# Layer 0 edge loop of a graph kernel: one-hots turned by TensorE in place of a broadcast of places, and the steps of three groups staggered in a fixed order

## Chip, cores and metric

One core of one Trainium2 chip. The time is the device time of one execution in microseconds (us); a time quoted for a kernel is the median of its timed runs. "Same" means within 2%.

The kernel before was met in two states. In the first comparison, whose chip is not on record, it took 7032 to 7043 us (four timed runs); in the first profile and in every later call, on the chips numbered 3, 4, 6 and 9, it took 6512 to 6539. I call them the slow and the fast state (the names are mine: the record compares the runs of one call only, and marks all of them fast). Numbers are only compared within one state.

## The reference

Four graph layers follow one another; the change touches only the first, a graph attention layer over 4096 nodes with 65536 edges (plus one self loop per node), 8 heads of 64 features:

```python
def _L0_gnn_ref(x, edge_index, W, a):
    ...
    h = jnp.einsum('nc,hcf->hnf', x, W)
    s_src = jnp.einsum('hnf,hf->hn', h, a_src)
    s_dst = jnp.einsum('hnf,hf->hn', h, a_dst)
    e = s_src[:, :, None] + s_dst[:, None, :]
    e = jnp.where(e > 0, e, ALPHA * e)
    e = jnp.where(adj[None, :, :], e, NEG_INF)
    att = jax.nn.softmax(e, axis=-1)
    out = jnp.einsum('hij,hjf->hif', att, h)
    out = jnp.transpose(out, (1, 0, 2)).reshape(N, H * F)
    return jax.nn.softmax(out, axis=1)
```

The kernel doesn't build the dense `att`. It walks the edges, sorted by source node, in 544 tiles of 128 edges. For each tile it gathers the rows of the far nodes, weighs them with exp(score), and adds them up by source node with a matmul against a one-hot matrix.

## The kernel before

The tiles go in 68 groups of eight. Cut to what the argument needs:

```python
def fetch(g):                        # GpSimd: eight indirect gathers, 4 groups of buffers
    rows = ep.tile([P, GT, DA], F32, name="rows", bufs=4)
    for j in range(GT):
        gather(rows[:, j, :D + H], htab, s_dst[:, at(g) + j:at(g) + j + 1])
    return rows

def fetch_places(g):                 # SyncE: the places of 1024 edges, broadcast to all partitions
    places = ep.tile([P, GT * P], BF16, name="places", bufs=3)
    nc.sync.dma_start(places, loc_rows[at(g):at(g) + GT].rearrange("t c -> (t c)").partition_broadcast(P))
    return places

def source_parts(g, places):
    oh_t = ep.tile([P, GT * P], BF16, name="oh_t")
    nc.vector.tensor_scalar(oh_t, places, col_i, None, op0=OP.is_equal)      # transposed one-hots
    e_ps = eps.tile([P, GT, 2, H], F32, name="e_ps")
    ...                              # ScalarE: four small copies `of`; PE: 24 score matmuls oh_t x of
    return e_ps

def weights(g, rows, u):             # DVE: the weights go into the row itself, then the one-hots
    nc.vector.tensor_mul(rows[:, :, D:D + H], u, s_new[...])
    return one_hots(ep, s_loc, at(g), GT)

def weigh(j, rows):                  # two heads on ScalarE, six on DVE
    two = rows[:, j:j + 2]
    ...
    g = two[:, :, :VH * F].rearrange("p t (h f) -> p t h f", h=VH)
    nc.vector.tensor_mul(g, g, two[:, :, D:D + VH].unsqueeze(3).to_broadcast([P, 2, VH, F]))

for g in range(-3, groups):
    ...                              # fetch(g+3), fetch_places(g+2), source_parts(g+1)
    for j in range(0, GT, 2):
        weigh(j, rows[g])
        if ps is not None:
            keep(g, j - 2, ps)       # DVE: acc += sum_ps
        ps = add_up(g, j, rows[g], done[g])      # PE: eight sum matmuls into sum_ps (two buffers)
        if j == 2:
            u = scores(rows[g + 1], e_ps)
    done[g + 1] = weights(g + 1, rows[g + 1], u)
    keep(g, GT - 2, ps)
```

`weigh` reads the rows and the weights. `one_hots` compares `row_i` with `s_loc`.

## Time and profile before

| | kernel before |
|---|---|
| timed, slow state | 7043.11 us (3 runs), with the run added later 7040.15 (4 runs) |
| profiled span, fast state | 6523.0 us, granted clock 0.966 |
| layer 0 loop, start of the first to start of the last gather | 277.5 to 1027.8: 750 us |

The lines of the profile that matter are in the prediction. A line of the groups view reads: line, engine, operation, names, shapes, count; then busy us and the mean ns of one; then idle time ahead of it and what ended that idle time.

### The profile page before, as it was taken

How to read it: one execution, taken by the hardware profiler on the slowest of the kernel's cores; microseconds unless marked ns; L12 is line 12 of the kernel's file. 1: busy time of each engine (PE TensorE's matmuls, PEld its weight loads, DVE VectorE, ACT ScalarE, POOL GpSimd, SP SyncE). 2: the span in 40 equal slices, each digit the busy share in tenths (PEclk: the TensorE clock that was granted, in tenths of full speed). 3: DMA queues.
4: the chain of work that ended last, by engine and by line, in shares of the span. 5: the costliest groups of instructions: out<-in, count | busy, mean ns of one | idle time of the engine just before them, and what ended most of it. 6: DMA issues, size and time to landing. Idle time of an engine off the chain costs nothing. (4 is left out here: it accounts for less than half of the span.)

```text
span 6523.0 us, 65629 instructions
## 1 busy us (share of the span) xinstructions
PE 5718.0 (88%) x18462; PEld 2778.4 (43%) x18462; DVE 4141.7 (63%) x7141; ACT 2937.3 (45%) x3977; POOL 3254.1 (50%) x3324
## 2 busy tenths in 40 slices
PE   6678887888779799999999999999999889978885
PEld 4366664322224344444444444444444365532221
DVE  7577778455443376676676776776766545556665
ACT  3244444300011277777777777777777533300001
POOL 1277772477760365555555555555555100037774
PEclk9899999999899899999999999999999899989998
DMA  8777775566774333333333333333333211137777
GB/s 225 182 220 214 218 215 176 162 201 203 195 214 175 125 109 103 102 98 104 101 98 105 101 98 102 103 98 106 100 98 104 82 45 62 59 106 209 210 209 243
DMA packets 399757, 926.39 MB, mean 142 GB/s; under 512 B 135926, under 2 KB 135926, under 8 KB 399382
## 3 DMA queue, kind: packets, MB, share of 16 engines
q0 software_dynamic: 230976, 721.66, 37.6%
q1 hardware_dynamic: 168406, 200.39, 9.6%
q8 instruction: 155, 2.54, 0.2%
q14 instruction: 220, 1.80, 0.1%
HBM read 818.71 MB, written 103.11 MB: 141 GB/s over the span
## 5 line engine op out<-in xcount | busy, mean ns | idle before, releaser
L438 PE MATMUL m_ps<-w_sb,h_t 128*128 128x512 f32 x4224 | 1905.9, 599 | 31.2 <-ACT h_t L957 31.2
L803 PE MATMUL sum_ps<-g,oh 128*128 128x512 f32 x2144 | 1146.9, 636 | 218.1 <-DMA g<-ztab,d_src 80.2
L438 PEld LDWEIGHTS m_ps<-w_sb,h_t 128*128 128x128 f32 x4224 | 771.1, 190 | 983.6 <-issue 791.2
L449 POOL DMA_INDIRECT qg<-qtab,eg x528 | 504.0, 954 | 990.6 <-ACT h_t L957 845.7
L449 POOL DMA_INDIRECT g<-ztab,d_src x528 | 501.4, 950 | 866.4 <-issue 811.6
L459 DVE TENSOR_TENSOR acc<-acc,sum_ps 128x512 f32 x800 | 550.2, 688 | 546.4 <-PE sum_ps L803 541.4
L803 PEld LDWEIGHTS sum_ps<-g,oh 128*128 128x128 f32 x2144 | 336.9, 191 | 1015.4 <-DVE acc L459 388.5
L449 POOL DMA_INDIRECT g<-ytab,s_dst x544 | 536.9, 987 | 353.2 <-DMA ytab<-acc 185.6
L914 POOL DMA_INDIRECT eg<-aug,d_eid x528 | 569.0, 1078 | 242.4 <-issue 131.0
L449 POOL DMA_INDIRECT rows<-htab,s_dst x544 | 585.9, 1077 | 204.9 <-issue 138.9
L957 ACT COPY h_t<-tr_ps 128x512 f32<-128x512 f32 x528 | 283.6, 589 | 777.6 <-PE tr_ps L955 777.6
L735 PE MATMUL sum_ps<-rows,oh 128*128 128x261 f32 x2176 | 551.5, 410 | 60.3 <-PE sum_ps L735 41.2
L449 POOL DMA_INDIRECT pg<-ptab,eg x528 | 508.7, 963 | 160.9 <-issue 160.6
L735 PEld LDWEIGHTS sum_ps<-rows,oh 128*128 128x128 f32 x2176 | 427.3, 202 | 163.3 <-PE sum_ps L735 66.3
L967 PE MATMUL small_ps<-z,oh 128*128 128x512 f32 x1056 | 477.8, 595 | 8.4 <-DVE z L1027 8.4
L1006 DVE TENSOR_TENSOR z<-m_ps,b_bc 128x512 f32<-128x512 f32 x132 | 91.3, 692 | 467.3 <-PE m_ps L438 467.3
L459 DVE TENSOR_TENSOR acc<-acc,small_ps 128x512 f32 x528 | 361.1, 684 | 31.8 <-PE small_ps L967 4.3
L1165 ACT ACTIVATE acc<-acc,dis 128x512 f32<-128x512 f32 x32 | 19.7, 706 | 671.2 <-DVEq L464 671.2
L1027 DVE TENSOR_TENSOR z<-z,t 128x1024 f32<-128x1024 f32 x264 | 310.4, 1217 | 8.2 <-ACTq L464 4.8
L992 DVE TENSOR_TENSOR z<-m_ps,b_bc 128x512 f32<-128x512 f32 x132 | 91.3, 692 | 352.6 <-PE m_ps L438 352.6
L967 PEld LDWEIGHTS small_ps<-z,oh 128*128 128x128 f32 x1056 | 201.5, 191 | 263.7 <-issue 221.9
L955 PEld LDWEIGHTS tr_ps<-ident,pg 128*128 128x128 f32 x2112 | 248.0, 142 | 151.1 <-issue 120.0
(248 smaller groups left out, 8389.5 us busy)
## 6 DMA issues: line engine op xcount, KB each, us to landing
aug<-row SPq DMA_DIRECT2D x32, 560.0 KB, 3.9
places<-loc_rows SPq DMA_DIRECT2D x68, 256.0 KB, 3.8
xt<-in_x_dram SPq DMA_DIRECT2D x16, 1024.0 KB, 5.7
row<-in_edge_attr_dram SPq DMA_DIRECT2D x32, 512.0 KB, 6.6
x<-xt SPq DMA_DIRECT2D x16, 1024.0 KB, 4.3
xt<-x SPq DMA_DIRECT2D x16, 1024.0 KB, 7.5
rows<-htab,s_dst POOLq DMA_INDIRECT x544, 3.8
g<-ytab,s_dst POOLq DMA_INDIRECT x544, 3.7
```

Source lines behind the costliest of these rows:

```text
L438: nc.tensor.matmul(ps, h_t[:, k, :], w_sb[:, k0 + k, :], start=start and k == 0, stop=stop and k == KC - 1)
L449: nc.gpsimd.indirect_dma_start(out=dst_ap, out_offset=None, in_=table, in_offset=bass.IndirectOffsetOnAxis(ap=idx, axis=0))
L459: nc.vector.tensor_add(into, into, ps)
L735: nc.tensor.matmul(ps[:, c, :HW], oh[:, j + k, :], rows[:, j + k, c * HW:(c + 1) * HW], start=k == 0, stop=k == 1)
L803: nc.tensor.matmul(ps, oh[:, j + k, :], g[:, j + k, :], start=k == 0, stop=k == pair - 1)
L914: nc.gpsimd.indirect_dma_start(out=eg[:, j // 2, (j % 2) * HALF:(j % 2 + 1) * HALF], out_offset=None, in_=aug.rearrange("e c -> (e c)").un ...
L955: nc.tensor.transpose(h_ps[:, k, :], h[:, j, k * P:(k + 1) * P], ident)
L957: nc.scalar.copy(h_t, h_ps)
L967: nc.tensor.matmul(ps, oh, m, start=True, stop=True)
L992: nc.vector.tensor_add(zz[:, 0, :], ps, b2_bc)
L1006: nc.vector.tensor_add(zz[:, 1, :], ps, b2_bc)
L1027: nc.vector.tensor_mul(mz[:, j:j + 2], mz[:, j:j + 2], t[:, j:j + 2])
```

## The change

The intent: no broadcast of places from memory and no second compare on DVE. PE turns the one-hots that exist anyway (they have to be made two groups ahead for that), ScalarE copies the result out of PSUM. So that the longer way doesn't stand in line, the steps of three groups are interleaved in one fixed order. The core of the diff (the removal of `loc_rows` and `col_i`, and a class that this loop doesn't call, are left out):

```diff
-            def fetch_places(g): ...
-            def source_parts(g, places):
-                oh_t = ep.tile([P, GT * P], BF16, name="oh_t")
-                nc.vector.tensor_scalar(oh_t, places, col_i, None, op0=OP.is_equal)
+            def turn(oh):
+                made = []
+                for j in range(0, GT, 4):
+                    t_ps = eps.tile([P, 4, P], F32, name="t_ps")
+                    for k in range(4):
+                        nc.tensor.transpose(t_ps[:, k, :], oh[:, j + k, :], ident)
+                    made.append(t_ps)
+                return made
+            def turned(g, made):
+                oh_t = ep.tile([P, GT, P], BF16, name="oh_t")
+                for j, t_ps in enumerate(made):
+                    nc.scalar.copy(oh_t[:, 4 * j:4 * j + 4, :], t_ps)
...
-            def weigh(j, rows):
+            def weigh_last(j, rows):          # the two heads on ScalarE, now a step of their own
...
-            for g in range(-3, groups): ...   # the order shown above
+            for g in range(-3, groups + 1):   # (the tests for the first and last groups are left out)
+                rows[g + 3] = fetch(g + 3)
+                made = turn(ohs[g + 1])
+                weigh(0, rows[g]);      sums[0] = add_up(g, 0, rows[g], ohs[g])
+                weigh_last(2, rows[g]); weigh(2, rows[g])
+                keep(g - 1, 6, sums.pop(6))
+                parts = turned(g + 1, made)
+                sums[2] = add_up(g, 2, rows[g], ohs[g])
+                weigh_last(4, rows[g]); weigh(4, rows[g]); keep(g, 0, sums.pop(0))
+                ohs[g + 2] = one_hots(ep, s_loc, at(g + 2), GT, 3)
+                e_ps = source_parts(*parts)
+                sums[4] = add_up(g, 4, rows[g], ohs[g])
+                u = scores(rows[g + 1], e_ps)
+                weigh_last(6, rows[g]); weigh(6, rows[g]); keep(g, 2, sums.pop(2))
+                sums[6] = add_up(g, 6, rows[g], ohs[g])
+                weights(g + 1, rows[g + 1], u); weigh_last(0, rows[g + 1])
+                keep(g, 4, sums.pop(4))
```

## The prediction

> **What bounds the kernel now.** The change touches only the edge loop of layer 0, so I first asked the view by tile where that loop stands. Its gathers of `rows` start between 277.5 and 1027.8 us of a profiled span of 6523.0 us; its last matmul starts at 1048.4. So at most some 770 us can move, and 2% of the timed 7043 us is 141 us, over a sixth of that. The loop handles 544 tiles as 68 groups of eight, and a group now takes (1027.8 - 277.5) / 543 x 8 = 11.05 us.
>
> Next the groups by line between 281 and 1040 us (count, then busy us, mean ns, and idle time before with what ended it):
>
> ```profile
> L449 POOL DMA_INDIRECT rows<-htab,s_dst x542 | 584.0, 1077 | 165.1 <-issue 138.6 <-PE sum_ps L735 9.4 <-DMA rows<-htab,s_dst 5.2
> L735 PE MATMUL sum_ps<-rows,oh 128*128 128x261 f32 x2144 | 544.0, 410 | 58.5 <-PE sum_ps L735 41.2 <-issue 7.6 <-PE e_ps L701 0.2
> L729 DVE TENSOR_TENSOR rows<-rows 128x768 f32<-128x768 f32 x268 | 249.8, 952 | 0.0
> L742 DVE TENSOR_TENSOR acc<-acc,sum_ps 128x522 f32 x268 | 186.1, 694 | 154.4 <-PE sum_ps L735 153.9
> L701 PE MATMUL e_ps<-of,oh_t 128*128 128x16 bf16 x1632 | 52.1, 170 | 114.4 <-DVE oh_t L693 103.7 <-DMA places<-loc_rows 10.5 <-ACT of L698 0.2
> L693 DVE TENSOR_SCALAR oh_t<-places,col_i 128x1024 bf16<-128x1024 bf16 x67 | 36.4, 543 | 0.0
> ```
>
> GpSimd's busy and idle time add up to 584.0 + 165.1 = 749.1 us: it is never free, because its idle time is the same 0.30 us after every gather (165.1 / 542). PE and DVE stand idle in turns: DVE 154 us for the sums, PE 104 us for `oh_t`. That is a chain through both engines, not one full engine.
>
> The timeline of one undisturbed group shows how the two fit (start, us, engine, what, idle time before):
>
> ```profile
> 327.89 0.94 POOL L449 DMA_INDIRECT rows<-htab,s_dst  x1 [0.30 <-issue]
> ...
> 328.18 1.22 DVE L444 TENSOR_TENSOR oh<-row_i,s_loc 128x1024 f32<-128x1024 f32 x1
> ...
> 329.32 0.69 DVE L742 TENSOR_TENSOR acc<-acc,sum_ps 128x522 f32 x1
> 329.93 0.54 DVE L693 TENSOR_SCALAR oh_t<-places,col_i 128x1024 bf16<-128x1024 bf16 x1
> 330.39 1.81 DVE L729 TENSOR_TENSOR rows<-rows 128x768 f32<-128x768 f32 x2
> 330.50 0.32 SPq L687 DMA_DIRECT2D places<-loc_rows  x1
> ...
> 330.52 1.62 POOL L449 DMA_INDIRECT rows<-htab,s_dst  x1 [0.30 <-issue]
> 330.52 0.76 PE L701 MATMUL e_ps<-of,oh_t 128*128 128x16 bf16 x24 [1.37 <-DVE oh_t L693]
> ...
> 331.43 3.76 PE L735 MATMUL sum_ps<-rows,oh 128*128 128x261 f32 x16
> 332.45 0.95 POOL L449 DMA_INDIRECT rows<-htab,s_dst  x1 [0.30 <-issue]
> 333.46 0.70 DVE L742 TENSOR_TENSOR acc<-acc,sum_ps 128x522 f32 x1 [1.27 <-PE sum_ps L735]
> ```
>
> Two things are to be seen. A gather takes 0.95 us, so 1.25 us from start to start and 10.0 us for eight; but the one that starts when SyncE has just issued the broadcast of `places` takes 1.62. This comes once in nearly every group I looked at (607.21, 641.52, 653.10, 663.78): GpSimd's plain group is 10.0 + 0.67 = 10.67 us. And the chain of PE and DVE has almost the same length: from `oh_t` at 652.39 and 663.19 the next turn is 10.8 us later, and inside it DVE waits 1.27 us for the first sum and 0.66 us for the third. The loop has two bounds of equal length. A change to one alone would give nothing; this change takes something from both.
>
> **What the Trainium skill says.** "DMA: Bandwidth & Descriptors", section "SWDGE vs HWDGE vs iDMA": descriptors of a DMA issued from GpSimd are computed in software by GpSimd itself, those of a DMA issued from SyncE by hardware; its part "Issuing engines are not separate DMA queues" says that both run on the same 16 DMA engines and interleave. The trace agrees as far as it goes: the broadcast costs GpSimd no instruction, yet the gather beside it takes 1.62 in place of 0.95 us. "TensorE: Matmul & The Clock Gate", "Part 4: PE-mode transpose": a 128x128 transpose takes about 275 ns in a kernel, its result goes to PSUM and needs a copy out. The transposes of layer 2 in this trace (L955) have a median of 273 ns, and pipelined 224.4 us / 1731 = 0.130 us each. The same page, "Part 1: The HAM clock gate": the PE clock falls to half after an idle window of some 3.4 us. Here the granted clock was 0.96 at 330 to 500 us and 0.94 at 500 to 900.
>
> **The change part by part.**
>
> *Removed.* 68 broadcasts of 256 KB: a group moves eight gathers of 128 x 520 x 4 bytes, 2.13 MB, and 0.26 MB of places, so 11% of the traffic goes. On GpSimd 68 x 0.67 = 46 us of stretched gathers go, and its floor falls to 10.0 us a group. On DVE 68 x 0.54 = 37 us of `oh_t` go. The one store of places in the sort (160 KB, one DVE cast) is under 1 us, off any wait that counts.
>
> *Added.* PE: 544 transposes x 0.130 = 71 us, 1.04 us a group. ScalarE: 136 copies of 128x512 out of PSUM; L957 in layer 2 is the same copy, 0.587 us, so 80 us, 1.17 a group. ScalarE has 347 us of work in 760, so the engine has room; whether the copies stand in a chain is a matter of order.
>
> *Moved.* The one-hots are made two groups ahead, transposes one group ahead; `keep` of a pair runs one or two pairs after its sum, the last in the next turn. I walk the new order with the spacings of the old timeline: a DVE `weigh` 0.89 us (0.87 to 0.91 start to start), `keep` 0.61 (0.70 until its end), one-hots 1.14, four score steps 0.87, weights 0.15; on PE eight sum matmuls 1.88 (3.76 / 2), turn 1.04, 24 score matmuls 0.76; 0.15 from PE to DVE and 0.1 back. DVE alone: 4 x 0.89 + 4 x 0.61 + 1.14 + 0.87 + 0.15 = 8.2 us. PE alone: 4 x 1.88 + 1.04 + 0.76 = 9.3 us. GpSimd: 10.0. The longest ring through the order: turn 1.04, sum 0 1.88, sum 2 1.88, score matmuls 0.76, to DVE 0.15, scores 0.87, weigh 6 0.89, keep 2 0.70, to PE 0.10, sum 6 1.88, and the next turn begins: 10.15 us. `keep 2` is in it because `sum_ps` has two buffers and sum 6 takes that of sum 2. Beside it, ScalarE's exp, filler copy and last weighting after the scores (0.26 + 0.19 + 1.01) end at nearly the same time as keep 2, so they are close to being in the ring too. The `oh_t` copies end some 2.4 us after the transposes, while PE does 3.76 us of sums: hidden.
>
> The same walk of the old order (oh_t to score matmuls 0.59, those and the gap 0.91, sum 1.88, to DVE 0.15, keep 0.62, scores 0.87, weigh 0.95, sum 4 1.98, to DVE 0.2, keep 0.6, weights 0.2, one-hots 1.14, keep 0.61) gives 10.7, which is what the trace has. So the plain group goes from 10.7 to about 10.2 us, the larger of 10.15 and 10.0.
>
> *Sum.* The mean group is 11.05, 0.36 over plain, from half-clock stretches of PE and gathers that stretch around them (612.89 to 618.52: 1.22, 1.58, 1.92 us). I keep that 0.36: 10.55. Saved: 0.50 x 68 = 34 us, if timed runs behave like the profiled one. They don't quite: they took 7043 where the profiled run took 6525, and no view tells why. If PE was slower in them, the new ring, with 7.4 us of PE in 10.2 (the old one with some 4.4 us in 10.7), loses more; I take a little off and say 31 us: 7012.
>
> **The rivals.**
> 1. *GpSimd and the gathers are the whole bound, and PE and DVE follow.* For: no free time on GpSimd, data that come just in time at the start (DVE waited 9.9 us for the first). Then a group is 10.0 + 0.36, or better since 11% of the traffic is gone: 0.7 x 68 = 47 us, about 6995. Against: DVE waited for `rows` only 6 times, 14.2 us in all.
> 2. *PE becomes the bound.* Its share goes from 8.3 to 9.3 us of a group, and at half clock every piece of the new ring doubles. With PE 20% slower the ring is 10.15 + 1.5 = 11.6, the old one 11.6 as well: no gain, 7043, or a few us of loss. Against: granted clock 0.94 and more here; and a denser PE should have fewer idle windows.
> 3. *The stagger meets an order fault*: ScalarE's last weighting after the scores, or the wait of keep 0 on the first sum, adds 0.5 us a group. Then 7040 to 7060.
>
> **Range and chances.** All of these lie within 20 to 60 us of one another, because 68 groups can each give at most some 1 us: faster by 2% would need 2.1 us a group, below GpSimd's floor of 10.0, and slower by 2% would need a group of 13.1. The range goes from rival 1 with some clock gain (6975) to no gain (7045). Faster 0.03, within 2% 0.95, slower 0.02.
>
> **What would show it.** Right: no gather of 1.62 us at a regular distance; GpSimd now idle for something other than issue, as buffers come free late; group pitch 10.3 to 10.7 us; the transposes near 0.13 us each; DVE idle about 2 us a group, before the scores and keep 0; last matmul of the loop near 1015 in place of 1048. Rival 1: pitch 10.4 with GpSimd still never free. Rival 2: PE above 90% busy in the loop and a lower granted clock. Rival 3: ScalarE named as the releaser of the sum matmuls. What would make me wrong: stretched gathers that stay without the broadcast, or a loop that moves by over 60 us either way.

## The result

Ratios here are the mean time of one kernel's fast runs over that of the other's of the same rounds, so they are not quite the ratio of the medians.

The changed kernel took 7233.11 us (7221.04 to 7255.48, four runs) against 7040.15 us (7032.43 to 7043.34, four runs): ratio 1.0279, 95% interval 1.0253 to 1.0306. It is slower, where I had given that a chance of 2%.

This comparison was made in the slow state. Later calls put both kernels on other chips. There the change took 6544.84 against 6528.68 us (1.0027, 1.0011 to 1.0044) and 6545.62 against 6520.28 (1.0041, 1.0012 to 1.0070): within 2%, but slower by some 20 us, and not faster by the 31 that I had predicted. So two questions have to be kept apart: why the expected gain is missing in the fast state, and what takes 193 us in the slow one. The experiments settle the first; the second stays open.

The change in the slow state, groups by line over its layer 0 loop (281 to 1370 us):

```profile
L772 PE MATMUL sum_ps<-rows,oh 128*128 128x261 f32 x2176 | 627.8, 443 | 346.4 <-issue 283.4 <-remote 59.4 <-PE sum_ps L772 2.1
L473 POOL DMA_INDIRECT rows<-htab,s_dst x544 | 556.4, 1023 | 550.7 <-PE sum_ps L772 358.8 <-issue 141.7 <-DVE node L684 43.4
...
L741 DVE TENSOR_TENSOR u<-e_ps,rows 128x64 f32<-128x64 f32 x68 | 15.3, 225 | 337.9 <-remote 260.8 <-PE sum_ps L772 56.0 <-DMA rows<-htab,s_dst 12.9
```

The same view of the same kernel in the fast state (281 to 1060 us):

```profile
L473 POOL DMA_INDIRECT rows<-htab,s_dst x539 | 606.2, 1125 | 164.3 <-issue 134.4 <-PE sum_ps L772 18.0 <-DMA rows<-htab,s_dst 4.0
L772 PE MATMUL sum_ps<-rows,oh 128*128 128x261 f32 x2143 | 547.4, 405 | 143.1 <-issue 125.7 <-PE sum_ps L772 9.2 <-DVE rows L766 8.2
...
L766 DVE TENSOR_TENSOR rows<-rows 128x768 f32<-128x768 f32 x270 | 251.3, 952 | 0.0
L779 DVE TENSOR_TENSOR acc<-acc,sum_ps 128x522 f32 x267 | 185.7, 696 | 88.2 <-PE sum_ps L772 86.3 <-DVE rows L751 1.0
L715 PE MATMUL t_ps<-ident,oh 128*128 128x128 f32 x535 | 82.0, 304 | 0.0
...
L723 ACT CAST oh_t<-t_ps 128x512 bf16<-128x512 f32 x134 | 73.0, 588 | 64.4 <-PE t_ps L715 64.0
```

Compare the fast-state POOL row with that of before in the prediction (584.0 us busy, mean 1077 ns, 165.1 idle). GpSimd is as full as it was: the idle time is again 164.3 / 539 = 0.30 us after every gather and nothing else. But the mean gather has grown from 1077 to 1125 ns, though the broadcast that I blamed for the long gathers is gone. In the slow state GpSimd waits 359 us for buffers, and DVE 261 us for a semaphore that the profile can't name ("remote").

The span of the loop says the same. Tile view, gathers of `rows`: count, shortest, median and longest in ns, start of the first and of the last. First the kernel before in the fast state:

```profile
L449 POOL DMA_INDIRECT rows<-htab,s_dst x544: 942/946/1941, 277.5 to 1027.8; - x182
```

The change in the fast state:

```profile
L473 POOL DMA_INDIRECT rows<-htab,s_dst x544: 942/949/1767, 274.6 to 1050.4; - x182
```

And the change in the slow state:

```profile
L473 POOL DMA_INDIRECT rows<-htab,s_dst x544: 940/946/1987, 280.0 to 1342.7; - x182
```

That is 750, 776 and 1063 us. In the fast state the loop loses 26 us and the rest of the kernel gains about 10, which leaves the 16 us of the first pair of medians.

### The profile page after: what moved, and what is told of

Same layout as the page of the kernel before. It is cut to its first block, busy times and chain, and to the rows that moved or that the text cites. A ratio compares the mean times of both kernels' runs of the same rounds, so it can differ in the third digit from the quotient of the medians.

```text
span 7253.6 us, 66642 instructions
## 1 busy us (share of the span) xinstructions
PE 5883.1 (81%) x19006; PEld 3015.2 (42%) x19006; DVE 4118.4 (57%) x7072; ACT 3030.9 (42%) x4113; POOL 3286.2 (45%) x3323
## 5 line engine op out<-in xcount | busy, mean ns | idle before, releaser
L858 PEld LDWEIGHTS sum_ps<-g,oh 128*128 128x128 f32 x2144 | 447.8, 220 | 1140.5 <-issue 611.6
L772 PE MATMUL sum_ps<-rows,oh 128*128 128x261 f32 x2176 | 627.8, 443 | 346.4 <-issue 283.4
L473 POOL DMA_INDIRECT rows<-htab,s_dst x544 | 556.4, 1023 | 550.7 <-PE sum_ps L772 358.8
L969 POOL DMA_INDIRECT eg<-aug,d_eid x528 | 589.7, 1117 | 244.3 <-issue 128.6
L772 PEld LDWEIGHTS sum_ps<-rows,oh 128*128 128x128 f32 x2176 | 459.6, 220 | 455.0 <-issue 280.0
L473 POOL DMA_INDIRECT pg<-ptab,eg x528 | 550.2, 1042 | 167.6 <-issue 160.6
L1061 DVE TENSOR_TENSOR z<-m_ps,b_bc 128x512 f32<-128x512 f32 x132 | 91.3, 692 | 476.4 <-issue 405.5
L779 DVE TENSOR_TENSOR acc<-acc,sum_ps 128x522 f32 x272 | 189.6, 697 | 182.2 <-PE sum_ps L772 169.1
```

Source lines behind the costliest of these rows:

```text
L473: nc.gpsimd.indirect_dma_start(out=dst_ap, out_offset=None, in_=table, in_offset=bass.IndirectOffsetOnAxis(ap=idx, axis=0))
L772: nc.tensor.matmul(ps[:, c, :HW], oh[:, j + k, :], rows[:, j + k, c * HW:(c + 1) * HW], start=k == 0, stop=k == 1)
L779: nc.vector.tensor_add(into, into, ps[:, :, :HW])
L858: nc.tensor.matmul(ps, oh[:, j + k, :], g[:, j + k, :], start=k == 0, stop=k == pair - 1)
L969: nc.gpsimd.indirect_dma_start(out=eg[:, j // 2, (j % 2) * HALF:(j % 2 + 1) * HALF], out_offset=None, in_=aug.rearrange("e c -> (e c)").un ...
L1061: nc.vector.tensor_add(zz[:, 1, :], ps, b2_bc)
```

## The experiments

Thirteen runs. All gave correct results.

### The two kernels again, on other chips

Edit: none. First the kernel before.

> The kernel before, unchanged, profiled again. Theory A (two states of the chip or of the recording: the first profile, 6523 us, was taken in a state in which the timed runs, 7040 us, never were): about 7040 us, clock near 0.91, sums and scores that wait several us longer than their matmuls last, semaphore records lost as in the profile after, and the unchanged loops of layers 1 and 3 as long as in the profile after (784 and 845 us from first to last gather, against 711 and 661 in the first profile). Its layer 0 loop is then some 190 us shorter than the 1063 us of the changed kernel. Theory B (the change itself slows everything): 6523 us again.

Measured: 6525.91 us, span 6524.1, clock 0.968; seven runs of the kernel before on that chip (number 9) lie between 6521.33 and 6529.88. The time of 7040 belongs to the first comparison (its chip, or something else about that call), not to the kernel alone.

Then the change.

> The changed kernel again, in the hope of a chip in the state of the first profile of before (before at 6523 us, clock 0.97). Theory A (the 190 us come from the order of steps, to which the state only adds): about 6600 to 6700, a group of 12 to 13.5 us, no semaphore records lost and no wait without a releaser. Theory B (the loss belongs to the state alone: PE's results reach the other engines several us late there, which the new order meets more often in its ring): before 6523, this about 6490, a group near 10.5 us, as predicted. If before is at 7040 again: 7233 again, and nothing is told apart.

Measured (chip 6): 6544.84 us (6537.62 to 6552.35) against 6528.68, ratio 1.0027. The 2.8% did not come back; they need the slow state.

### One part of the change alone

Turning by TensorE, but the steps in the old order:

```diff
-            for g in range(-3, groups + 1): ...   # staggered
+            for g in range(-3, groups):
+                parts = turned(g + 1, turn(ohs[g + 1]))
+                for j in range(0, GT, 2):
+                    weigh(j, rows[g])
+                    ...                            # keep(j - 2), add_up(j), as before
+                    if j == 0: e_ps = source_parts(*parts)
+                    if j == 2: u = scores(rows[g + 1], e_ps)
```

> The steps in the old order, one-hots made a group earlier and turned by TensorE in place of the broadcast. If the turning (PE work, ScalarE copies, one more hop between engines) costs the 190 us: about 7200 or more. If the stagger does: about 7000 to 7040.

Measured: 6694.21 us against 6523.34, ratio 1.0258 (1.0241 to 1.0275); the loop takes 900 us. The timeline of one group (start, us, engine, what, idle time before it) shows why:

```profile
599.91 0.23 ACT L695 COPY of<-node 128x48 bf16 x1 [0.44 <-issue]
...
600.86 0.23 ACT L695 COPY of<-node 128x48 bf16 x1 [0.72 <-issue]
601.00 2.02 ACT L727 ACTIVATE rows<-rows 128x64 f32<-128x64 f32 x8
...
601.63 1.19 PE L736 MATMUL sum_ps<-rows,oh 128*128 128x261 f32 x4 [2.16 <-ACT rows L727]
...
602.85 0.70 DVE L743 TENSOR_TENSOR acc<-acc,sum_ps 128x522 f32 x1 [3.69 <-PE sum_ps L736]
```

In this trace ScalarE does its work in the order of the program: the two copies out of PSUM and the four `of` copies stand ahead of the weighting of two heads (L727), and the first sum matmul waits for that. This group loses 2.2 us on PE and 3.7 on DVE there; over the loop PE waits 127.5 us for these rows. Turning is only cheap if the order hides it, and that is what the stagger is for.

The stagger alone, with the broadcast and the compare on DVE kept:

```diff
-                for j, t_ps in enumerate(made):
-                    nc.scalar.copy(oh_t[:, 4 * j:4 * j + 4, :], t_ps)
+                nc.vector.tensor_scalar(oh_t..., places, col_i, None, op0=OP.is_equal)
...
-                    made = turn(ohs[g + 1])
+                    places[g + 2] = fetch_places(g + 2)
```

> The staggered order of the changed kernel, but with the broadcast of places and the DVE comparison, no turning. If the stagger costs the 190 us: about 7200. If the turning does: about 7000 to 7050.

Measured: 6573.70 us, ratio 1.0072 (1.0055 to 1.0089); the loop takes 808 us. The groups view of its loop:

```profile
L481 POOL DMA_INDIRECT rows<-htab,s_dst x544 | 643.7, 1183 | 209.2 <-issue 133.5 <-ACT of L729 43.7 <-PE sum_ps L774 14.9
```

The 43.7 lie before the first gather. So GpSimd is again never free, yet its mean gather is 1183 ns, the longest of all. The new order makes gathers longer, with the broadcast or without it. That sent me back to the gathers.

### What makes a gather long

In the prediction I took the long gather to be slowed by the broadcast that SyncE issues beside it. In the change there is no broadcast. Its gathers in the fast state, beside the DVE work around them:

```profile
606.92 0.95 DVE L766 TENSOR_TENSOR rows<-rows 128x768 f32<-128x768 f32 x1
...
607.12 1.58 POOL L473 DMA_INDIRECT rows<-htab,s_dst  x1 [0.30 <-issue]
...
609.00 0.95 POOL L473 DMA_INDIRECT rows<-htab,s_dst  x1 [0.30 <-issue]
609.21 1.82 DVE L766 TENSOR_TENSOR rows<-rows 128x768 f32<-128x768 f32 x2
610.25 1.60 POOL L473 DMA_INDIRECT rows<-htab,s_dst  x1 [0.30 <-issue]
...
611.74 0.95 DVE L766 TENSOR_TENSOR rows<-rows 128x768 f32<-128x768 f32 x1
...
612.15 1.35 POOL L473 DMA_INDIRECT rows<-htab,s_dst  x1 [0.30 <-issue]
```

The first weigh ends at 606.92 + 0.95 = 607.87, and the gather that started inside it ends at 608.70, 0.83 us later. The second gather that started inside a weigh ends at 611.85, 0.82 after the end of the pair (611.03); the third at 613.50, 0.81 after 612.69. The gather at 609.00, which was under way when a weigh began, takes its plain 0.95.

Over the whole loop of this run I sorted the 544 gathers by the DVE operation under way at their start. Of the 172 that started inside a weigh, 90% end 0.81 to 0.82 us after the end of the weigh (5th to 95th percentile), with a mean duration of 1.395 us. The 67 that started in the one-hots have a mean of 1.147, the 145 in `keep` 0.963, the 131 with DVE idle 0.947. Of before: 123 in a weigh, mean 1.438; 66 in the one-hots, 1.097; 144 in `keep`, 0.946; 153 idle, 0.946. What the two bad operations have in common is that both inputs lie in SBUF.

That is not the only way to hold a gather. In the run with the stagger alone, five gathers started while nothing but the `oh_t` compare ran on DVE, which reads one tensor from SBUF. They too end 0.82 us after it, and the longest took 1.12 us (at 435.03). In the kernel before no gather started so.

The Trainium skill has this, on pages that the prediction did not use. "SBUF — State Buffer", section "SBUF: two separate sides", says that VectorE and GpSimd share a port pair as an exclusive lock for the whole instruction, taken among others by a VectorE operation with two SBUF inputs against a GpSimd operation that reads SBUF (the gather takes its row numbers from `s_dst`, in SBUF); "GPSIMD Engine Reference", section "1. Specifications", names the contention in a line of its table. The trace agrees, with the 0.82 us beside it. In the old timeline the end of `oh_t`, the broadcast's issue (330.50) and the start of a weigh (330.39) fall together in each group, so that the wrong one could be blamed.

The theory can be tried from both sides. First the broadcast: double it, in the kernel before, the second copy unread.

```diff
                 nc.sync.dma_start(places, loc_rows[...].partition_broadcast(P))
+                again = ep.tile([P, GT * P], BF16, name="again", bufs=2)
+                nc.sync.dma_start(again, loc_rows[...].partition_broadcast(P))
```

> The kernel before with the broadcast of places sent twice, the second copy read by nobody. The step of the prediction (the broadcast stretches the gather beside it by 0.67 us): two stretched gathers a group, 117 us of stretch in place of 71, a group of 11.7 us, 6570 where before is at 6525. Theory C: stretch 71 us and 6525, within 10 us.

Measured: 6568.22 us, ratio 1.0068 (1.0051 to 1.0085). It costs 43 us, but not in the gathers. Groups view, and from the view of waits the one that is new (us in total, times, longest):

```profile
L449 POOL DMA_INDIRECT rows<-htab,s_dst x544 | 574.6, 1056 | 253.9 <-issue 140.8 <-PE sum_ps L737 52.8 <-ACT of L700 44.1
```

```profile
DVE oh_t L695 <- DMA places<-loc_rows: 39.3, 6, 11.9
```

The mean gather is 1056 ns, shorter than the 1077 of before. Most of the 43 us are six waits of `oh_t` for `places` that came late, 39.3 us in all, five of them at 382 to 455 us. A broadcast costs something when it comes late; it doesn't stretch gathers.

Now the other side: take the second SBUF input away. The weights are written to spare room of the `e_ps` bank too, and weigh reads them from there. In the change:

```diff
-                e_ps = eps.tile([P, GT, 2, H], F32, name="e_ps")
+                e_ps = eps.tile([P, 3, GT, 2 * H], F32, name="e_ps")
...
+                w = e_ps[:, 1, :, :H]
+                nc.vector.tensor_mul(w, u, s_new[...])          # beside the same product into rows
...
-                nc.vector.tensor_mul(g, g, two[:, :, D:D + VH].unsqueeze(3).to_broadcast([P, 2, VH, F]))
+                nc.vector.tensor_mul(g, g, w[:, j:j + 2, :VH].unsqueeze(3).to_broadcast([P, 2, VH, F]))
```

> The changed kernel, with the weights of the heads read from PSUM by the DVE multiplication of the rows, in place of from SBUF; same work, same order. Theory C (a gather that starts while DVE runs an operation with two inputs in SBUF is held up; in the profiles a gather that starts in the multiplication of the rows is stretched by 0.46 us on the mean, one that starts in a sum out of PSUM by 0.00): the stretched gathers go from 97 us in all to 15 to 30 us (the one-hots keep theirs), a group from 11.4 to 10.3 to 10.6 us, and 6470 to 6500 us where before is at 6525. Theory D (the stretch comes from something else, DMA traffic or the granted clock): 6545 as before. Should the chip be one where before takes 7040, the shares of stretched gathers still tell.

Measured: 6489.42 us (6485.32 to 6492.99) against 6524.89, ratio 0.9949 (0.9932 to 0.9965). That is "same" by the 2% rule, but clear of noise it is faster than both kernels, though it has one more DVE operation a group. Tile view of its gathers:

```profile
L473 POOL DMA_INDIRECT rows<-htab,s_dst x544: 942/946/1994, 280.1 to 1000.0; - x182
```

The loop takes 720 us in place of 776. All of the 137 gathers that start in a weigh take 0.94 to 0.95 us; the 64 that start in the one-hots take 1.539 on average.

The same edit in the kernel before (its one-hots and order unchanged):

> The same edit in the kernel before. Theory C with the second bound of my prediction (PE and DVE need 10.7 us a group in the old order anyway): stretched gathers from 71 to under 25 us, but only 0.3 to 0.4 us a group saved: 6498 to 6510 where before is at 6525. If GpSimd is the only bound: 10.3 us a group, 6475. Theory D: 6525.

Measured: 6543.96 us (6529.33 to 6560.84), ratio 1.0041 (1.0020 to 1.0062). Groups view of its loop:

```profile
L449 POOL DMA_INDIRECT rows<-htab,s_dst x541 | 527.6, 975 | 204.7 <-issue 141.1 <-PE sum_ps L737 51.0 <-DMA rows<-htab,s_dst 6.1
```

The gathers did get shorter, 975 ns for 1077, and by their starts the loop goes from 750 to 735 us. But that is not a gain. GpSimd only runs further ahead, and now waits for buffers that PE's sums free (51.0 us). By its sums the loop is as long as before. Tile view of the kernel before, then of this run:

```profile
L735 PE MATMUL sum_ps<-rows,oh x2176: 381/383/782, 294.9 to 1048.4; 128*128 128x261 f32 x198
```

```profile
L737 PE MATMUL sum_ps<-rows,oh x2176: 381/383/795, 294.1 to 1047.8; 128*128 128x261 f32 x198
```

That is 753.5 and 753.7 us, 11.1 us a group with the stretch and without it. So the old order has a second bound, the chain of PE and DVE, and it is as tight as the first, as the prediction said. (In the fast runs with the new order, gathers and sums give the same loop within 2 us.) In this run 45 of the 67 turns from group to group had the full clock and took 10.8 us; the 22 with a mean granted clock under 0.9 took 11.9.

In the kernel before, the gather that the prediction looked at starts 22 to 32 ns after the broadcast's issue in each group from 309 to 998 us, though groups last 10.7 to 12.3 us. So its stretch seems to have followed the chain rather than set the pace; that is argued from these numbers, not shown. The time of this run rose by 19 us; its profiled run was the fastest, at 6529, and where the others lost I did not find.

Last, the change with the one-hots relieved as well: eight columns of places are copied into PSUM (0.16 us), and the one-hots read them there (for 66 of the 68 groups; the branch for the first two is left out).

```diff
-                    ohs[g + 2] = one_hots(ep, s_loc, at(g + 2), GT, 3)
+                    spot = parts_of.pop(g)[:, 2, 0, :GT]        # spare room in e_ps of group g
+                    nc.vector.tensor_copy(spot, s_loc[:, at(g + 2):at(g + 2) + GT])
+                    ohs[g + 2] = one_hots(ep, spot, 0, GT, 3)
```

> The change with the weights read from PSUM (as in the run of 6489 us) and with the one-hots reading their places from PSUM too, so that neither the weigh nor the one-hots has two inputs in SBUF in this loop. The theory that a gather is held by VectorE only while an operation with two SBUF inputs runs expects that no group of gathers that start beside the one-hots is stretched any more (40 us of stretch in that run, all of it there), the mean gather near 0.96 us, GpSimd's group at 10.0 to 10.3 us, the layer 0 loop at 685 to 710 us and the time at 6455 to 6480 us (ratio 0.990 to 0.994). The rival, that what holds the gather is any long VectorE operation on SBUF (the one-hots still write 4 KB a partition), expects the 40 us of stretch to stay and the time within 5 us of 6489.

Measured: 6450.99 us (6450.04 to 6456.17) against 6528.85, ratio 0.9886 (0.9868 to 0.9903). Timeline, with a gather starting inside the one-hots and two inside weighs:

```profile
599.91 1.22 DVE L468 TENSOR_TENSOR oh<-row_i,e_ps 128x1024 f32<-128x1024 f32 x1
...
600.03 0.94 POOL L473 DMA_INDIRECT rows<-htab,s_dst  x1 [0.30 <-issue]
...
602.48 0.95 DVE L769 TENSOR_TENSOR rows<-rows,e_ps 128x768 f32<-128x768 f32 x1
602.53 0.95 POOL L473 DMA_INDIRECT rows<-htab,s_dst  x1 [0.30 <-issue]
...
604.83 1.81 DVE L769 TENSOR_TENSOR rows<-rows,e_ps 128x768 f32<-128x768 f32 x2
605.03 0.95 POOL L473 DMA_INDIRECT rows<-htab,s_dst  x1 [0.30 <-issue]
```

And the tile view:

```profile
L473 POOL DMA_INDIRECT rows<-htab,s_dst x544: 942/946/1268, 278.3 to 957.7; - x182
```

One gather of 544 is over 1.05 us. The loop takes 679 us, 10.01 us a group: eight gathers at 1.25 us and nothing beside. GpSimd's issue of gathers is now the whole bound of this loop.

This is the best version, 1.1% faster than the kernel before in the same call (within 2%, so "same" by the rule), and by the ratios of separate calls 1.4% faster than the change. The rival of this run, that any long DVE operation on SBUF holds a gather, is out: the one-hots still write 4 KB to each partition.

### Looking for the slow state

Edit: none. These runs were to find a chip in the slow state, since no profile of the kernel before exists from there.

> The kernel before, unchanged, for one look. Two states of chip have been seen: one in which it takes about 6525 us and one in which it takes about 7040. If this run falls in the second, its profile is the first of the kernel before there: the theory that each hand-over from TensorE to VectorE comes some us late in that state expects its layer 0 loop well over the 750 us of the first state (850 to 1000), with VectorE waiting for remote semaphores and a clock near 0.92; the rival, that the state only slows TensorE's own instructions, expects the waits to be as in the first state and only the durations longer. In the first state: 6515 to 6535 us and nothing new.

> The change, unchanged, beside the kernel before on the same chip. In the first state: ratio 1.000 to 1.005 as in the earlier repeat. In the second: ratio 1.02 to 1.035 as in the first result, and a layer 0 loop near 1060 us.

> The kernel before, unchanged, for one look, in case this call falls on a chip in the slower state: there 7030 to 7050 us, and by the theory of late hand-overs a layer 0 loop of 850 to 1000 us. Otherwise 6515 to 6535 us and a loop of 750 us.

> The kernel before once more, for one look, only to have its profile if the call falls on a chip in the slower state, of which no profile of the kernel before exists. There the theory of late hand-overs from TensorE to VectorE expects 7030 to 7050 us, a layer 0 loop of 850 to 1000 us and waits of VectorE for remote semaphores in it. On a chip in the first state: 6515 to 6535 us, and the question stays open.

> The kernel before, for one look. On a chip in the slower state: 7030 to 7050 us, and by the theory of late hand-overs from TensorE to VectorE a layer 0 loop of 830 to 1000 us with VectorE waiting for remote semaphores; by the rival, that only TensorE's own pace falls there, a loop with the waits of the first state and longer matmuls. On a chip in the first state: 6515 to 6535 us, and the question stays open.

Measured: 6520.94 us for the kernel before, 6545.62 for the change (1.0041; 1.0012 to 1.0070), then 6529.47, 6526.07 and 6522.26 for the kernel before. All in the fast state, so these runs only repeat it.

What there is of the slow state is the trace of the change. One hand-over in it:

```profile
713.25 0.75 PE L735 MATMUL e_ps<-of,oh_t 128*128 128x16 bf16 x24
...
713.85 2.01 PE L772 MATMUL sum_ps<-rows,oh 128*128 128x261 f32 x8
...
719.07 0.23 DVE L741 TENSOR_TENSOR u<-e_ps,rows 128x64 f32<-128x64 f32 x1 [5.55 <-remote]
...
721.61 3.82 PE L772 MATMUL sum_ps<-rows,oh 128*128 128x261 f32 x8 [5.75 <-issue]
```

By the record, PE has done the score matmuls at 714.0; DVE begins with them at 719.07, and PE's next sum waits 5.75 us for what follows. In the fast state the wait ahead of the same `u` is for data or sums, 134 us in all, against 338 here. PE's granted clock suffers too. Per kernel from 276 to 1100 us (busy time and count of PE, PE's weight loads, DVE, ScalarE and GpSimd, then clock, DMA share, GB/s), the change in the slow state, which is inside its loop all that time, while the other three leave theirs between 973 and 1068 us, so that these rows compare only roughly:

```profile
276.00:1100.00 824.00, 547.66 (x3224) 446.04 (x3224) 417.62 (x705) 316.88 (x1202) 433.52 (x423) 0.81 0.50 137
```

The change in the fast state:

```profile
276.00:1100.00 824.00, 657.22 (x4377) 540.75 (x4376) 588.76 (x1036) 438.06 (x1662) 609.98 (x543) 0.92 0.67 185
```

The kernel before in the fast state:

```profile
276.00:1100.00 824.00, 631.12 (x3888) 486.94 (x3888) 638.51 (x1155) 356.13 (x1548) 585.87 (x544) 0.92 0.72 210
```

And the last version, change and both operands in PSUM:

```profile
276.00:1100.00 824.00, 707.83 (x4636) 557.15 (x4637) 678.13 (x1384) 480.14 (x1761) 514.94 (x544) 0.96 0.72 206
```

Code that the change doesn't touch is longer in the slow state as well: the gathers `g<-ytab` of layer 1 span 1535.4 to 2319.1 us there (784 us) against 1233.2 to 1941.6 (708), those of layer 3 (`g<-ztab`) 845 against 664 us. So the state is not made by the change; the change only loses more in it. How much of that is in the loop is an estimate: if the rest of the kernel loses alike in both kernels, the change adds 193 us in all and had gained some 10 us outside the loop, so about 200 us of the loop's 1063 are its own, and the kernel before would stand at about 860 there.

It is argued, not shown, that the new order is more sensitive because each group passes more results from PE to another engine one after the other (turn, sums, scores, sum 6) with no time to spare. Whether the matmuls or only their signals came late, the records don't tell; some signals are missing from that trace ("remote", "issue"). That stays open.

## Why the prediction was wrong

Measured by the starts of its gathers, the loop can be put together from three terms. A plain group is 8 x 1.25 = 10.0 us. The stretch of the gathers is their busy time less 0.947 us each; the third is the time that GpSimd waits for buffers. The sum fits by construction: the table sorts the time, and what causes it was shown by the experiments. Per group, in us (fast state unless noted):

| kernel | gathers over 1.05 us | stretch | waits for buffers | 10.0 + both | measured |
|---|---|---|---|---|---|
| before | 131 | 1.04 | 0.01 | 11.05 | 11.05 |
| change | 189 | 1.41 | 0.01 | 11.42 | 11.43 |
| stagger alone | 231 | 1.89 | 0.01 | 11.90 | 11.91 |
| turning alone, old order | 99 | 0.81 | 2.43 | 13.24 | 13.26 |
| before, two broadcasts | 105 | 0.87 | 0.65 | 11.52 | 11.54 |
| before, weights in PSUM | 25 | 0.22 | 0.59 | 10.81 | 10.83 |
| change, weights in PSUM | 54 | 0.59 | 0.00 | 10.59 | 10.61 |
| change, weights and places in PSUM | 1 | 0.00 | 0.01 | 10.01 | 10.01 |
| change, slow state | 82 | 0.60 | 5.03 | 15.63 | 15.66 |

By the prediction's own steps:

- *The bound.* "GpSimd is never free" was right for both kernels in the fast state. "The loop has two bounds of equal length. A change to one alone would give nothing" was right too: with 55 us of stretch taken from the kernel before, its sums still took 754 us.
- *The failed step in the fast state.* "On GpSimd 68 x 0.67 = 46 us of stretched gathers go, and its floor falls to 10.0 us a group." The stretch was not the broadcast's. A gather that starts while DVE runs a weigh or the one-hots, with two SBUF inputs, ends only 0.82 us after that operation. With the broadcast gone 189 gathers were still over 1.05 us (99 in the old order), and the doubled broadcast added none. The new order put 172 gathers into a weigh where the old one had 123, and the stretch rose from 70.7 to 96.1 us. In place of -46 us the term was +25, and in the new order the gathers are the bound: with both operands in PSUM the loop falls from 776 to 679 us.
- *The failed step in the slow state.* "The longest ring through the order ... 10.15 us" reckons 0.15 us for the way from PE to DVE. In the slow trace a group took 15.66 us. DVE stood idle 338 us ahead of `u`, 5.0 us a group, where the change in the fast state has 2.0; the hand-over shown above takes 5.07. Why is open.
- *The residue.* "I keep that 0.36", laid to PE's half clock and to gathers that stretch around it, was half right. In the old order it stays without the stretch (11.1 us a group by the sums, 10.8 at full clock). In the new order it need not be kept: the last version runs at 10.01.
- *The costs of the parts.* Right. ScalarE's copies took 588 ns (587 predicted), the transposes 82.0 / 535 = 0.153 us each in the loop (0.130 predicted; 0.134 in the last version). Both are hidden by the stagger, and not without it (900 us).
- *The new ring.* 10.15 us was a little long: in the last version the loop runs at 10.01 us with GpSimd never waiting, so the ring is no longer than that. Once the stretch is gone, the change gives what it was made for.
- *Rival 1* named the bound rightly, and gave it 47 us of gain, because it too counted on shorter gathers. *Rival 2* reckoned both rings at 11.6 us with PE 20% slower; at a clock of 0.81 the change took 15.66, so by that reckoning PE's own pace does not account for it. *Rival 3* was not met in the change in the fast state, but it is what the run with the old order showed (PE waits 127.5 us for ScalarE).
- *The signs.* I had written that stretched gathers that stay without the broadcast would make me wrong; that is what happened. The last sum matmul of the loop starts at 1067 us in the fast state, for the 1015 expected.
- *The chances.* "Slower by 2% would need a group of 13.1": in the fast state that holds (11.43). The first comparison had 15.66, from waits of 5.03 us a group that the fast state doesn't have. I had seen that timed runs and profile differed by 520 us, wrote "no view tells why", and took off 3 us for it. A gap of 8% between the profile and the times is a risk to a verdict at 2%, and should have gone into the chances.

## What to carry to other kernels

Where GpSimd issues gathers back to back, look at the DVE operation under way at the start of each long one: here operations with two SBUF inputs held it until their end, and the one-input compare did so too. Moving the small operand to PSUM took all of that away in this loop, for two small DVE operations a group. Check such a gain at the end of the loop's work, not by the engine that runs ahead: the same edit in the old order shortened the gathers' part by 15 us and the loop by none. And when one kernel's timed runs and its profile differ by several per cent, predict for two states or widen the range: here the change lost 193 us in one state and some 20 in the other.

## What the Trainium skill lacked or had wrong

- "SBUF — State Buffer", section "SBUF: two separate sides": it has no figure for what the lock costs an indirect gather; the page's nearest one, about 115 ns after the end of the DVE operation, was taken with a `tensor_copy`. Here the gather ends 0.81 to 0.82 us after the DVE operation does (0.947 us alone), and the longest that started in a weigh of 0.95 us took 1.63 in the kernel before.
- The same section: it says that the one that starts first has the pair for the whole instruction and the other fully blocks. A weigh does hold a gather to its end. But a gather held a weigh only in its first 0.04 us: in the kernel before, the weighs that began 0 to 10 ns into a gather took 979 to 990 ns, those that found no gather under way 946 on average, and those that began 0.13 us or more into one 949. With one input in PSUM the first kind took 941 to 946 ns (last version, 0 to 9 ns). The gather itself was not lengthened.
- "GPSIMD Engine Reference", section "1. Specifications": it names the contention but not the way out, which "SBUF — State Buffer" does name. One input in PSUM is enough: in the last version 182 gathers started in such a weigh and 66 in such one-hots, with a mean of 0.946 us each.
- "DMA: Bandwidth & Descriptors", section "SWDGE vs HWDGE vs iDMA": it has no figure for a broadcast issued by SyncE beside gathers issued by GpSimd. It did not lengthen them here: with two broadcasts a group the mean gather was 1056 ns, with one 1077, and those that found DVE idle took 945 and 946.
- No page that I read has the two states: the same kernel at 6525 and at 7040 us on one core, in different calls.
